# An attention and experts kernel on one core: rank products for two tiles at once, layernorms in two placed steps, a later last route, another order of the last blocks

## The chip, the cores and the metric

The kernel runs on one core of one Trainium2 chip, in fp32. The metric is the device time of one execution in microseconds (us), as a median over runs. One execution was also recorded by the hardware profiler; all durations of single instructions come from it.

The engines are called as in the profile: PE is TensorE (matmuls and transposes; PEld are its weight loads), DVE is VectorE, ACT is ScalarE, POOL is GpSimd, SP issues most DMAs.

## The reference

`x` holds 2048 tokens of 256 channels. The result is two residual layers one after the other (cut to what matters; `layernorm` has no weights where none are shown):

```python
x = x + layernorm(long_block(layernorm(x)))
x = x + layernorm(experts(layernorm(x)))

def long_block(x):                                  # 16 heads of 16 channels
    h  = layernorm(x) * ln1w + ln1b
    xc = silu(causal_depthwise_conv(h, conv_w, 4 taps) + conv_b)
    q, k = l2norm(h @ Wq), l2norm(h @ Wk)           # per head
    v = layernorm(h @ Wv) * vnw + vnb               # per head
    u = sigmoid(xc @ Wig + big) * k * v
    mem = scan(m = gamma * m + u), gamma = sigmoid(xc @ Wg + bg)    # over the tokens
    o = (layernorm(mem) * mnw + mnb) * q            # per head
    o = (layernorm(o) * gnw + gnb) * sigmoid(xc @ Wog + bog)
    h = x + o @ Wo
    h2 = layernorm(h) * ln2w + ln2b
    return h + (silu(h2 @ Wgate) * (h2 @ Wval)) @ Wout              # 1024 inner channels

def experts(x):                                     # 8 experts of 176 inner channels, the best 2 of each token
    shared = (silu(x @ sw_gate) * (x @ sw_up)) @ sw_down            # 704 inner channels
    top_w, top_i = top_k(softmax(x @ router_w.T), 2); top_w /= sum(top_w)
    routed = sum over j of top_w[j] * expert[top_i[j]](x)
    return routed + sigmoid(x @ shared_gate_w) * shared
```

## The kernel before

The tokens are taken in 8 blocks (`NB`) of 256, each of two tiles (`NT`) of 128 tokens. Channels are two groups (`KC`) of 128. A product in fp32 of 256 columns is two PE instructions of 0.216 us. The kernel has three stages.

**Attention and perceptron (0 to about 418 us).** The work of a block is cut into generators, each of which does one step and yields:

- `enter`: statistics of `x`, two scales from them by POOL's power (the reference's two layernorms in a row are one here), and `ln1` by ACT.
- `project`: the transposed `hT`, the convolution `xc`, then `q`, `k_`, `v`, their norms (`rsqrt` by bit tricks on DVE, lines 218 to 224), two POOL multiplies of `v` (L392, L393), `v` times `k_` (L395), and three gates on PE and ACT (L410).
- `remember`: transposes of `v`, the scan, transposes back, norm of `o`, two POOL operations (L449, L450), `o` times `q` (L451), and a second norm (to L459).
- `leave`: the product with `w_o`, the residual `h1`, its layernorm `ln2` and `h2T`.
- `perceptron`: eight steps `f`, each two products into a PSUM tile psM, `hid` by ACT's silu (L520) and DVE's multiply (L521), and the product of the `hid` of two steps before into the sum psD (L510). After them `h1` plus the sum, its layernorm, and `y += h1` on POOL (L531).
- `route`: layernorm `ln3` of the first layer's result, its transposes `yT`, the router's logits, the best two experts (`chosen`), the rank of each token within its expert by a product with the triangular matrix `earlier` and with `ones`, the `rows` from it, and four scatters to `xs` in DRAM by POOL (L617).
- `shared`: the expert that all tokens use: six steps into `shid` (ACT L651, DVE L652, the last half one L658), two products with `s_down`. In this stage for blocks 0 to 3.

What order these steps are issued in is written out by hand. `turns` gives every part an offset in blocks and a list of places, one for each step, in units of which a block has 8 (`NF`); all steps are sorted by `(b + first) * NF + place` and issued in that order. A block period is about 40 us. `enter` of the next block is not in the list: it is issued after a certain step of `project`, and held behind that step's last instruction. The framework's scheduler may still move single instructions; within an engine the final order is fixed, and the engine works through it in order.

**Routed blocks (to about 535 us).** `tables` and `fill` set up offsets, then `shared(4)`, then 39 `routed` blocks of 128 rows: load of `xb` from `xs`, transposes `xT` (DVE L736), products with the weights `m_w` of the expert that a register gives, and a scatter to `ys` by POOL (L765).

**The end.** `fetch` brings each token's two expert results `g` back (16 DMAs of 256 KB). PE computes `shared` of blocks 5, 6 and 7, ACT writes them to `f` with the gate. DVE adds the two weighted expert results (`combine`, L785), then comes a layernorm and the residual (`finish`, L800) and the output DMA, in the order of the blocks 0 to 7. `turn(b)` does the finish of block b-1 and then the sums of block b.

Lines 230, 231 are the statistics of any layernorm, 235 its `nb` (minus mean times scale, on DVE), 241 and 242 POOL's sum and power for the scale, 248 ACT's normalising, 285 transposes and 294 products.

## Time and profile before

| | |
|---|---|
| median of 3 runs | 592.75 us (592.64 to 594.23) |
| the profiled execution | 592.66 us |
| its span (first to last instruction) | 590.9 us |
| TensorE's granted clock, mean | 0.974 |
| PE busy | 534.9 us, 91% of the span |
| DVE, ACT, POOL busy | 327.3, 224.7, 196.8 us |

The page's second part cuts the span into 40 slices of 14.8 us, with the busy share of each engine in tenths. The waits list says which engine stood idle, for how long in total, how many times, and for what. In the timeline every row is one instruction or a run of equal ones: start, duration, engine, line, operation, output and inputs, and in brackets the idle time just before it with what ended that. The chain of waits follows the work that ended last back from the end; what stands in it sets the end. The windows give for each stretch its length, the busy time of PE, PEld, DVE, ACT and POOL with the number of instructions, then the granted clock, the DMA share and the GB/s.

### The profile page before, as it was taken

What the parts mean: (1) busy time and instruction counts of PE and PEld (TensorE: products, weight loads), DVE (VectorE), ACT (ScalarE), POOL (GpSimd) and SP (SyncE); (2) the same over time, 40 slices, a digit from 0 to 9 for tenths busy, and PEclk for the clock granted to TensorE, in tenths of its full rate; (3) what the DMA queues carried; (4) which work ended last, traced back from release to release, by engine and by line L of the source; (5) the groups of instructions that cost most, each with busy time, mean ns of one, the idle gap of its engine ahead of it and who ended that gap; (6) DMA issues with size and microseconds to landing.
All of it is one profiled execution on the core that took longest, in us unless ns stands there. A gap on an engine that the chain in (4) does not pass through costs nothing.

```text
span 590.9 us, 8088 instructions
## 1 busy us (share of the span) xinstructions
PE 534.9 (91%) x2564; PEld 448.3 (76%) x2564; DVE 327.3 (55%) x1069; ACT 224.7 (38%) x527; POOL 196.8 (33%) x307
## 2 busy tenths in 40 slices
PE   2895699999898998999999999996999999999991
PEld 1674578788787886888888888885877777768881
DVE  3588878577587586785753323223333333333684
ACT  2654353362553443543233222222223444432432
POOL 4224333324445254353412314114203333331111
PEclk9988889999999999999999999998999999999997
DMA  6940000000010010000100640001333333315311
GB/s 190 358 139 0 1 2 1 0 1 1 2 36 2 0 37 0 6 32 2 37 0 1 200 130 20 18 1 36 109 89 95 98 98 96 106 59 180 141 54 53
DMA packets 29822, 35.87 MB, mean 61 GB/s; under 512 B 4737, under 2 KB 24660, under 8 KB 29782
## 3 DMA queue, kind: packets, MB, share of 16 engines
q1 hardware_dynamic: 26082, 26.93, 14.7%
q0 software_dynamic: 3408, 8.43, 4.1%
q8 instruction: 21, 0.34, 0.3%
q14 instruction: 19, 0.16, 0.1%
q10 hardware_dynamic: 292, 0.01, 0.0%
HBM read 22.72 MB, written 13.55 MB: 61 GB/s over the span
## 4 chain that ended last, share of the span: by engine, by line
PE 34%; DVE 26%; POOL 16%; issue 11%; DMA 5%; ACT 5%; SPq 1%; POOLq 1%; ACTq 0%; DVEq 0%
PE psM L294 12%; PE psA L294 8%; PE psD L510 6%; POOL ys L765 4%; PE psS L294 4%; DVE ln_st L230 3%; DVE f L785 2%; POOL ln_rs L242 2%; DMA ys<-yb,pair 2%; POOL v L392 2%; DVE xc L359 2%; POOL v L393 2%; DVE ss L278 1%; DVE rw L222 1%; DVE rw L223 1%
## 5 line engine op out<-in xcount | busy, mean ns | idle before, releaser
L510 PE MATMUL psD<-w_out,hid 128*128 128x256 f32 x256 | 66.4, 391 | 7.7 <-DVE hid L521 7.5
L294 PE MATMUL psM<-h2T,w_gate 128*128 128x256 f32 x256 | 67.2, 385 | 0.4 <-DVE lg L570 0.4
L294 PE MATMUL psM<-h2T,w_val 128*128 128x256 f32 x256 | 65.7, 379 | 0.0
L510 PEld LDWEIGHTS psD<-w_out,hid 128*128 128x128 f32 x256 | 49.0, 194 | 18.0 <-DVE hid L521 11.5
L765 POOL DMA_INDIRECT ys<-yb,pair x39 | 38.4, 984 | 72.8 <-ACT yb L764 48.2
L294 PE MATMUL psM<-m_w,xT 128*128 x156 | 52.9, 462 | 2.4 <-DVE xT L736 2.4
L294 PEld LDWEIGHTS psM<-h2T,w_val 128*128 128x128 f32 x256 | 48.7, 190 | 7.9 <-issue 1.4
L294 PEld LDWEIGHTS psM<-h2T,w_gate 128*128 128x128 f32 x256 | 47.5, 192 | 7.1 <-DVE lg L570 1.4
L521 DVE TENSOR_TENSOR hid<-hid,psM 128x256 f32<-128x256 f32 x64 | 26.0, 413 | 37.1 <-ACT hid L520 37.1
L520 ACT ACTIVATE hid<-psM 128x256 f32<-128x256 f32 x64 | 23.8, 382 | 58.4 <-PE psM L294 58.3
L294 PE MATMUL psD<-m_w,hT 128*128 x156 | 40.2, 380 | 0.0
L617 POOL DMA_INDIRECT xs<-ln,rows x32 | 32.2, 1005 | 23.9 <-DVE rows L613 10.0
L738 DVE TENSOR_SCALAR pair<-xb,of 128x1 int32<-128x1 f32 x39 | 10.6, 272 | 48.3 <-DMA ys<-yb,pair 43.8
L294 PE MATMUL psA<-yT,s_gu 128*128 128x256 f32 x144 | 36.5, 394 | 0.0
L241 POOL TENSOR_SCALAR ln_rs<-ln_mv 128x2 f32<-128x2 f32 x24 | 6.6, 274 | 87.4 <-DVE ln_mv L231 87.3
L294 PEld LDWEIGHTS psM<-m_w,xT 128*128 128x128 f32 x156 | 26.7, 190 | 11.2 <-issue 1.5
L294 PE MATMUL psA<-xc,w_io 128*128 128x256 f32 x104 | 26.6, 401 | 5.3 <-ACT xc L363 5.1
L294 PEld LDWEIGHTS psA<-yT,s_gu 128*128 128x128 f32 x144 | 27.4, 198 | 3.3
L294 PEld LDWEIGHTS psD<-m_w,hT 128*128 128x128 f32 x156 | 26.7, 190 | 2.3 <-ACT yb L764 0.3
L749 ACT ACTIVATE padded<-psM 128x176 f32<-128x176 f32 x39 | 12.4, 317 | 41.1 <-PE psM L294 39.1
L294 PEld LDWEIGHTS psA<-xc,w_io 128*128 128x128 f32 x104 | 20.7, 201 | 8.9 <-ACT xc L363 5.9
L277 ACT ACTIVATE sq<-o 128x512 f32<-128x512 f32 x16 | 10.1, 630 | 41.5 <-DVE o L271 41.5
(233 smaller groups left out, 1128.8 us busy)
## 6 DMA issues: line engine op xcount, KB each, us to landing
xb<-xs SPq DMA_DIRECT2D x39, 129.0 KB, 2.1
g<-ys SPq DMA_DIRECT2D x16, 256.0 KB, 5.2
xs<-zeros SPq DMA_DIRECT2D x16, 129.0 KB, 5.1
x<-in_L_attn_x_dram SPq DMA_DIRECT2D x8, 256.0 KB, 3.5
out_dram<-f SPq DMA_DIRECT2D x8, 256.0 KB, 2.1
m_w<-in_L_ffn_w_gate_dram SPq DMA_DIRECT2D x2, 704.0 KB, 7.6
m_w<-in_L_ffn_w_up_dram SPq DMA_DIRECT2D x2, 704.0 KB
w_gate<-in_L_attn_Wgate_dram SPq DMA_DIRECT2D x1, 1024.0 KB, 8.1
```

The lines of the kernel that those rows point to most:

```text
L230: nc.vector.bn_stats(st[:, n, :], src[:, n, :])
L242: nc.gpsimd.tensor_tensor(rs, rs, neg_half, ALU.pow)
L294: nc.tensor.matmul(po, lhs[i], rhs[i], start=(i == 0), stop=(i == len(lhs) - 1))
L359: made = nc.vector.scalar_tensor_tensor(xc[:, k, :], hT[:, k, j : j + TB], conv_w[:, k, j : j + 1], xc[:, k, :], ALU.mult, ALU.add,)
L392: nc.gpsimd.tensor_tensor(heads(v), heads(v), over_heads(head_rows["vnw"]), ALU.mult)
L393: nc.gpsimd.tensor_tensor(heads(v), heads(v), over_heads(head_rows["vnb"]), ALU.add)
L510: nc.tensor.matmul(total[:, n * C : (n + 1) * C], hids[f][:, tok(n)], w_out[:, f, :], start=False, stop=(f == NF - 1 and n == NT - 1),)
L520: nc.scalar.activation(hid, po[:, 0:TB], AF.Silu)
L521: nc.vector.tensor_tensor(hid, hid, po[:, TB:], ALU.mult)
L617: inst = nc.gpsimd.indirect_dma_start(out=xs, out_offset=bass.IndirectOffsetOnAxis(ap=rows[:, c : c + 1], axis=0), in_=ln[:, n, :], in_off ...
L749: nc.scalar.activation(h[:, 0:I], po[:, 0:I], AF.Silu)
L765: inst = nc.gpsimd.indirect_dma_start(out=ys, out_offset=bass.IndirectOffsetOnAxis(ap=pair, axis=0), in_=yb, in_offset=None, bounds_check= ...
```

## The change

Five things are changed.

1. In `route` the rank product takes `chosen` and `seen` of both tiles at once, 16 columns in place of twice 8.
2. A layernorm is two functions: `scale_of` has the statistics and POOL's scale, `normalize` has `nb` on DVE and ACT's normalising. In `leave`, `perceptron` and `route` there is a yield between, so that each half has a place of its own. `enter` has such a yield too and becomes a part of `turns`. `v` times `k_` becomes a step of its own; `o` times `q` moves into the step after. A table `early` gives other places to a few steps of the first blocks.
3. The last block's `route` has places later by more than a unit for the transposes and what follows.
4. Three steps of `shared(5)` are issued before the routed blocks (`AHEAD`).
5. In the end phase the blocks are summed in the order 5, 0, 1, 6, 2, 3, 7, 4. For blocks 5 to 7 the experts' parts come first (the first by ACT into `f`, the second by DVE), and the shared part is added by DVE from PSUM. `finish` has two steps. The last block is finished in halves of 128 tokens, with two DVE operations in place of `nb`, ACT and an addition, and an output DMA for each half.

The core of the diff:

```diff
+    def behind(engine):
+
+        traced = nc.cur_bb.bb.instructions
+        return tc.issue_after(next(i for i in reversed(traced) if i.engine == engine))
+
+    def scale_of(part, src):
+
+        mv = stats(part, src)
+        nt = src.shape[1]
+        rs = small.tile([P, nt], F32, tag=f"rs{part}", name="ln_rs")
         nc.gpsimd.tensor_scalar(rs, mv[:, :, 1], EPS, None, ALU.add)
-        nc.gpsimd.tensor_tensor(rs, rs, neg_half, ALU.pow)
-        offset(nb, mv, rs)
-        return rs, nb
-
-    def normalize(dst, src, rs, nb):
-        for n in range(NT):
+        nc.gpsimd.tensor_tensor(rs, rs, neg_half[:, 0:nt], ALU.pow)
+        return mv, rs
+
+    def normalize(part, dst, src, mv, rs):
+
+        nt = src.shape[1]
+        nb = small.tile([P, nt], F32, tag=f"nb{part}", name="ln_nb")
+        nc.vector.scalar_tensor_tensor(nb, mv[:, :, 0], -1.0, rs, ALU.mult, ALU.mult)
+        for n in range(nt):
             nc.scalar.activation(
                 dst[:, n, :], src[:, n, :], AF.Identity, bias=nb[:, n : n + 1],
                 scale=rs[:, n : n + 1],
             )
-
-    def layernorm(part, dst, src):
-
-        rs, nb = scale_of(part, stats(part, src))
-        normalize(dst, src, rs, nb)
...
-        mv = stats("L", xt)
+        with behind(DVE) if b else ExitStack():
+            mv = stats("L", xt)
...
-        made = offset(nb, mv, inner)
-        ln = att.tile([P, NT, C], F32, tag="ln1", name=f"ln1_{b}", bufs=5)
-        normalize(ln, xt, inner, nb)
 
         nc.gpsimd.tensor_scalar(sc[:, 0, :], mv[:, :, 1], EPS, None, ALU.add)
-        nc.gpsimd.tensor_tensor(sc[:, 0, :], sc[:, 0, :], neg_half[:, 0:NT], ALU.pow)
+        nc.gpsimd.tensor_tensor(sc[:, 0, :], sc[:, 0, :], neg_half, ALU.pow)
         back = small.tile([P, NT], F32, tag="back", name=f"back_{b}", bufs=5)
         nc.gpsimd.tensor_tensor(back, va, inner, ALU.mult)
         nc.gpsimd.tensor_tensor(back, back, sc[:, 0, :], ALU.mult)
+        yield
+        ln = att.tile([P, NT, C], F32, tag="ln1", name=f"ln1_{b}", bufs=5)
+        normalize("L", ln, xt, mv, inner)
         live[b].update(ln=ln, back=back)
-        yield "entered", made
...
-        made = nc.vector.tensor_tensor(v, v, k_, ALU.mult)
-        yield "norms", made
+        yield
+        nc.vector.tensor_tensor(v, v, k_, ALU.mult)
+        yield
...
+        yield
         nc.vector.tensor_tensor(o, o, t["q"], ALU.mult)
-        yield
...
-        layernorm("B", ln, h1)
+        mv, rs = scale_of("B", h1)
+        yield
+        normalize("B", ln, h1, mv, rs)
...
-        layernorm("M", h1, h1)
+        mv, rs = scale_of("M", h1)
+        yield
+        normalize("M", h1, h1, mv, rs)
...
+    KEEP_FROM, LATE_FROM, AHEAD = 4, 5, 3
...
-        layernorm("R", ln[:, :, 0:C], x_tiles[b])
+        mv, rs = scale_of("R", x_tiles[b])
+        yield
+        normalize("R", ln[:, :, 0:C], x_tiles[b], mv, rs)
...
-        for n in range(NT):
-            product(pr[:, n * E : (n + 1) * E], [earlier, ones], [chosen[:, n, :], seen[:, n, :]])
+        product(pr[:, 0 : NT * E], [earlier, ones], [chosen, seen])
...
+            if b < LATE_FROM:
+                nc.scalar.activation(f_[:, n, :], pn, AF.Copy, scale=gate)
+            else:
+                nc.vector.scalar_tensor_tensor(
+                    f_[:, n, :], pn, gate, f_[:, n, :], ALU.mult, ALU.add
+                )
+            yield
...
-    def combine(b, g):
-
-        wt, f_ = live[b]["wt"], part_of[b]
-        for n in range(NT):
-            for j in range(TOPK):
-                nc.vector.scalar_tensor_tensor(
-                    f_[:, n, :], g[n][:, j, :], wt[:, n, j : j + 1], f_[:, n, :],
-                    ALU.mult, ALU.add,
-                )
-        mv = stats("R", f_)
-        rs = small.tile([P, NT], F32, tag="rsR", name=f"rs_{b}")
-        nb = small.tile([P, NT], F32, tag="nbR", name=f"nb_{b}")
-        nc.gpsimd.tensor_scalar(rs, mv[:, :, 1], EPS, None, ALU.add)
-        nc.gpsimd.tensor_tensor(rs, rs, neg_half, ALU.pow)
-        offset(nb, mv, rs)
-        return rs, nb
-
-    def finish(b, rs, nb):
-        f_ = part_of[b]
-        normalize(f_, f_, rs, nb)
-        nc.vector.tensor_tensor(f_, f_, x_tiles[b], ALU.add)
-        nc.sync.dma_start(in_tokens(y_out, b), f_)
+    def combine(b, n, g):
+
+        f_ = part_of[b][:, n, :]
+        for j in range(TOPK):
+            share = live[b]["wt"][:, n, j : j + 1]
+            if b >= LATE_FROM and not j:
+                nc.scalar.activation(f_, g[n][:, j, :], AF.Copy, scale=share)
+            else:
+                nc.vector.scalar_tensor_tensor(f_, g[n][:, j, :], share, f_, ALU.mult, ALU.add)
+
+    def finish(b, halves):
+
+        scales = [(hs, *scale_of("R", part_of[b][:, hs, :])) for hs in halves]
+        yield
+        for hs, mv, rs in scales:
+            f_ = part_of[b][:, hs, :]
+            normalize("R", f_, f_, mv, rs)
+            nc.vector.tensor_tensor(f_, f_, x_tiles[b][:, hs, :], ALU.add)
+            nc.sync.dma_start(in_tokens(y_out, b)[:, hs, :], f_)
+
+    def finish_last(b, n):
+
+        f_ = part_of[b][:, n : n + 1, :]
+        mv, rs = scale_of("R", f_)
+        nc.vector.tensor_scalar(f_[:, 0, :], f_[:, 0, :], mv[:, 0, 0:1], None, ALU.subtract)
+        nc.vector.scalar_tensor_tensor(
+            f_[:, 0, :], f_[:, 0, :], rs[:, 0:1], x_tiles[b][:, n, :], ALU.mult, ALU.add
+        )
+        nc.sync.dma_start(in_tokens(y_out, b)[:, n : n + 1, :], f_)
...
-        (route, 4, (0, 3.7, 4.8, 4.9, 9.2, 10.2, 10.3)),
-        (leave, 2, (0.6, 2.6, 2.8, 5.2)),
-        (remember, 1, (0.5, 2.1, 3.1, 4.1)),
-        (project, 0, (0.2, 0.3, 1.2, 1.4, 2.2, 3.1, 3.3, 3.5, 4.5, 5.5, 5.5)),
-        (perceptron, 3, (*range(NF), 7.8, 7.9)),
+        (route, 4, (1.4, 2.0, 4.2, 5.2, 5.3, 9.2, 10.2, 10.3)),
+        (leave, 2, (0.6, 2.6, 2.8, 3.6, 5.2)),
+        (remember, 1, (0.5, 2.1, 3.1, 4.3)),
+        (project, 0, (0.2, 0.3, 1.2, 1.4, 2.2, 3.1, 3.3, 4.3, 3.5, 4.5, 5.5, 5.5)),
+        (enter, -1, (3.6, 4.6)),
+        (perceptron, 3, (*range(NF), 7.8, 7.9, 8.6)),
         (shared, NB, evenly(NS + 4)),
     )
+
+    early = {(enter, 1): (0.25, 0.35), (enter, 2): (0.4, 1.3), (remember, 1): (2.5, 4.1, 5.1, 6.1)}
+    early[route, NB - 1] = (1.4, 2.0, 5.6, 6.6, 6.7, 7.9, 7.9, 7.9)
...
-        what, made = next(run, None) or (None, None)
-
-        if what == ("first", "conv", "norms")[min(b, 2)] and b + 1 < NB:
-            with tc.issue_after(made.ins):
-                next(enter(b + 1))
+        next(run, None)
...
+    late = {b: shared(b, all_banks) for b in range(LATE_FROM, NB)}
+    for _ in range(AHEAD):
+        next(late[LATE_FROM])
...
-    fetched = [fetch(b) for b in range(NB)]
-    scales = []
-
-    def turn(b):
-        if b:
-            finish(b - 1, *scales[b - 1])
-        if b < NB:
-            scales.append(combine(b, fetched[b]))
-
-    done = 0
+
+    order = (5, 0, 1, 6, 2, 3, 7, 4)
     for b in range(LATE_FROM, NB):
-        for step, (_, made) in enumerate(shared(b, all_banks)):
-            while done < b and 3 * done + 4 <= (NS + 3) * (b - LATE_FROM) + step:
-                with ExitStack() as held:
-                    for m in made:
-                        held.enter_context(tc.issue_after(m.ins))
-                    turn(done)
-                done += 1
-    for b in range(done, NB + 1):
-        turn(b)
+        new_part(b)
+    fetched = {b: fetch(b) for b in order}
+    jobs = []
+    ends = []
+    for b in order:
+        for n in range(NT):
+            jobs.append(lambda b=b, n=n: combine(b, n, fetched[b]))
+            if ends:
+                jobs.append(ends.pop(0))
+        if b < LATE_FROM:
+            run = finish(b, [slice(0, NT)])
+            ends += [lambda run=run: next(run, None)] * 2
+    jobs = iter(jobs + ends)
+
+    def work():
+        next(jobs, lambda: None)()
+
+    ends = []
+    for b in range(LATE_FROM, NB):
+        for step, _ in enumerate(late[b]):
+            for run in ends:
+                next(run, None)
+            work()
+            if step % 4 == 3:
+                work()
+            if b == NB - 1 and step > NS:
+                finish_last(b, step - NS - 1)
+        ends.append(finish(b, [slice(0, NT)]))
```

## The prediction

> **What bounds the kernel now.** I read the page's slices first, then the PE's waits, then the timeline and the chain of waits around each large gap. The profiled execution took 592.66 us (span 590.9 and 1.76 around it), the median of the three runs is 592.75: the same within 0.3% (1.8 us), which is about what a measurement of this kernel can tell from no change. So the sums are made against 592.66.
>
> ```profile
> PE 534.9 (91%) x2564; PEld 448.3 (76%) x2564; DVE 327.3 (55%) x1069; ACT 224.7 (38%) x527; POOL 196.8 (33%) x307
> PE   2895699999898998999999999996999999999991
> PEclk9988889999999999999999999998999999999997
> ```
>
> TensorE is the bound, and nothing else is near it on average. From 275 to 400 us it has no gap. So there are three sources of gain: PE work removed, PE gaps (start, 43-78, one at each block's end to 234, 406, the end), and slices at a lower clock. The PE's waits say who ends the gaps:
>
> ```profile
> PE psS L285 <- DVE v L395: 8.1, 3, 3.3
> PE psD L510 <- DVE hid L521: 7.5, 7, 1.9
> PE psA L294 <- ACT xc L363: 5.1, 1, 5.1
> PE psM L285 <- ACT ln L248: 4.6, 1, 4.6
> PE psM L294 <- DVE xT L736: 2.4, 2, 1.3
> ```
>
> The second row is the gap that recurs at a block's end. The timeline at block 2's end shows its cause:
>
> ```profile
> 185.54 0.69 DVE L395 TENSOR_TENSOR v<-v,k 128x512 f32<-128x512 f32 x1 [1.59 <-POOL v L393]
> 188.42 0.16 DVE L235 SCALAR_TENSOR_TENSOR nb<-ln_mv,sc 128x2 f32<-128x2 f32 x1 [1.02 <-POOL sc L314]
> 190.65 0.41 DVE L521 TENSOR_TENSOR hid<-hid,psM 128x256 f32<-128x256 f32 x1
> 191.12 2.33 PE L510 MATMUL psD<-w_out,hid 128*128 128x256 f32 x5 [1.87 <-DVE hid L521]
> ```
>
> DVE works in order. It waits for POOL twice (1.59 for `v`, 1.02 for the power in `enter`) with the perceptron's `hid` behind both, and PE, which has no other work issued ahead, waits for `hid`. The same picture stands at 110-113, 151 and 233 us.
>
> **Rank products (less PE work).** Eight instructions each of these rows become four with 16 columns:
>
> ```profile
> L294 PE MATMUL psM<-chosen,earlier x4: 172/256/257, 417.2 to 417.7; 128*128 128x8 f32 x4
> L294 PE MATMUL psM<-seen,ones x4: 256/256/256, 417.3 to 417.9; 128*128 128x8 f32 x4
> ```
>
> They took 0.81 us at 395.58 and 0.90 at 280.28, some 0.1 us per instruction, which is the pace of weight loads and not of columns. Half as many with doubled columns: 0.40. Gain 8 x 0.45 = **3.5 us**, all on the bound (2.0, where a gap follows the product anyway, to 3.6).
>
> **Start and first blocks.** Before, block 1's statistics stood on DVE and POOL between block 0's statistics and its `nb`: the power L314 ran at 9.95 behind block 1's `va` (8.89). With `enter` a turn of its own the power comes about 0.7 earlier, DVE's other setup ending at 10.09 allows no more: **0.7**. In 43-58 us the multiplies of `v` come ahead of `o` on POOL: `v` times `k` at about 47.5 instead of 51.19, but `o` times `q` at 51 instead of 49.6, and the silu of `xc` that ends the 5.31 us gap at 57.7 some 0.8 earlier: **0.8** (0 to 4 for both).
>
> **Block ends.** The layernorm's first half (statistics, `rs`) and second half (`nb`, ACT) become separate places, so that `nb` is issued when POOL is done; `v` times `k` is a later step, as is `o` times `q`. Moved with `enter` are per block two statistics pairs on DVE, six POOL instructions, `nb` and two ACT normalises; no DMA. Retiming block 2 by the durations of its rows: `v` times `k` at 184.85 (still waiting for POOL L393, whose place hardly moves), no wait for `nb`, the hids of f 5, 6, 7 at 187.3, 190.75 and 191.1. `hid` 6 is then late because ACT has `th` and two gates ahead of it: that is the next stall. PE ends block 2's psD at 192.9, 3.85 after f 7's products (189.08) instead of 5.24. **1.2 in each of four blocks, 4.8** (0 if ACT is fully the next wait, 9 if all gaps close).
>
> Here the Trainium skill speaks against the change. The row first: POOL's multiply of `o` and DVE's two-input operation beside it.
>
> ```profile
> 176.50 1.30 POOL L449 TENSOR_TENSOR o<-o,mnw 128x512 f32<-128x512 f32 x1 [0.94 <-DVE ss L385]
> 176.71 1.18 DVE L222 TENSOR_TENSOR rw<-rkv 128x64 f32<-128x64 f32 x1
> 179.53 0.23 DVE L222 TENSOR_TENSOR rw<-rkv 128x64 f32<-128x64 f32 x1
> ```
>
> The same DVE operation takes 1.18 beside POOL and 0.23 alone. "SBUF — State Buffer", section "Who interferes with whom", says that a DVE instruction with two SBUF inputs and a GpSimd instruction that reads SBUF shut each other out for the whole instruction. By the rule, moving DVE work ahead under POOL's two multiplies of `v` (1.28 each) blocks one such operation a block by about 1.0 and leaves 0.2 of the 1.2: the sum would be 4.0 smaller. By the row, DVE stands idle for that `v` anyway (1.59) and `hid` has only one SBUF input: I take 4.8.
>
> **The clock.** TensorE's granted clock was half from 191.3 to 194.7, and twelve psD instructions took 4.54 there instead of 2.6. "TensorE: Matmul & The Clock Gate", Part 1, "What's actually happening", gives an idle window of some 3.4 us as what halves the clock, free-running. The gap here was only 1.87 long, and gaps as long at 151 and 233 were followed by the full clock. By the rule shortening a 1.9 gap gains nothing more; by the row it gains up to 1.9. I take **1.0**.
>
> **The last route.** The chain of waits at 400-407:
>
> ```profile
> 403.45 0.96 POOL xs L617
> 404.43 0.26 POOL ln_rs L241
> 404.77 0.73 POOL ln_rs L242
> 405.72 0.61 ACT ln L248
> 406.37 0.48 PE psM L285
> ```
>
> POOL issues three scatters before block 7's `ln_rs`, and PE stands from 401.65 to 406.37 (4.72). POOL's order stays, and so does this date; but the step with ln3's transposes now comes after all six of `shared(3)`'s remaining products, about 2.5 us of PE work moved into the gap: **2.5**, with some of the half clock that follows (406.4-409.8): **0.8** (0 to 1.7). Scatters and fill behind the route start when `chosen` is there, neither earlier nor later.
>
> **Routed blocks.** Three chunks of `shared(5)` (12 products, 24 instructions of 0.216: 5.18 us) go ahead of the first expert block. Their cover is the 1.44 gap at 434.85, where PE waits for DVE's `xT`: **0.9**; the rest is only moved from the end. If the cover is gone it costs nothing, as the work is due anyhow; from 0 to 1.3, and below nothing by 0.3 if one of the three `shid` multiplies that come along (0.30 each on DVE) stands just ahead of `xT`.
>
> **The end.** Windows by stage:
>
> ```profile
> 540.00:579.00 39.00, 37.76 (x174) 32.25 (x172) 27.03 (x84) 14.44 (x33) 6.76 (x14) 1.00 0.37 133
> 579.00:591.00 12.00, 0.00 (x0) 0.00 (x0) 4.67 (x12) 2.32 (x5) 0.92 (x2) 0.70 0.19 66
> ```
>
> PE ends at 578.83, and 12.1 us follow in which two blocks' sums, a layernorm in six waits and the output DMA (4.7 after DVE's end) stand in a row. After: the last expert block ends at T (534.62 before); the first `g` lands at T+7.9, as before. PE has 87 products of 0.432 left, 37.6 us. DVE has from the first `g` 26 weighted sums x 0.40 (10.4), six from PSUM (2.6, ACT's before), statistics 7.9, `nb` 0.9, residual adds 4.5, `shid` 4.7, the last halves 1.4: 32.4 us, against 29.7 that PE has left then. So DVE is nearly the bound, and `shid`, in order behind sums, holds up `s_down` of block 6 by about 3.3 (1.23 before). PE ends at T+40.9, then the last half's sum 0.45, statistics 0.65, the two POOL operations with their hand-overs 1.25, one multiply-add 0.45, with 1.0 of other DVE work, and the DMA 4.7: T+49.4, where it was T+56.3. That is 6.9, of which 5.18 was only moved ahead: **1.7**; I take 1.2, as the sixteen `g` now land in another order. Cost at nothing: six first sums that move to ACT against six evictions that leave it (14.44 busy of 39), and a ninth output DMA on SP, hidden behind the first half's. From -1.5 (DVE fully the bound) to +5 (no stall).
>
> Sum: 3.5 + 1.5 + 4.8 + 1.0 + 3.3 + 0.9 + 1.2 = 16.2, and 592.66 - 16.2 = **576.5 us**.
>
> **Rivals.**
> *Gains in part*: DVE bounds the end (-1.5) and ACT's `th` and gates take the place of the `nb` wait (0 instead of 4.8, no clock gain). 16.2 - 2.7 - 4.8 - 1.0 = 7.7: 585.0. For: ACT has `hid` 6 behind four others. Against: one of POOL's two waits does go.
> *All gaps close*: block ends 9, first blocks 4, clock 1.9 and 1.7, no stall at the end: about 568. Against: `v` times `k` waits for POOL still.
> *Slower*: `enter`'s six POOL instructions (187.23-189.50, 2.27 us) now stand ahead of `v`'s two multiplies. They wait for DVE's statistics; my retiming leaves 1.3 us to spare. If the statistics come late, `v` times `k` and all hids behind it come later in each of six blocks. The 11.4 us that the other parts gain are used up from 1.9 us a block. At 2.6 it gives 592.66 - 11.4 + 15.6 = 597. Against: the statistics are tied to a DVE instruction well before.
> *No change*: gaps that go come back before the next product, and the end is bounded by DVE: 592 to 593.
>
> **How the numbers follow.** Forecast 0.62 (own range 572 to 581), gains in part 0.2, all gaps 0.08, slower 0.06, no change 0.04. Faster by over 0.3%: the first three less a little, 0.88; same 0.05; slower 0.07. The range, 568 to 587, leaves out the two last and the edges.
>
> **What would show it.** Right: rank rows x16 columns with half the count; no DVE wait for `nb` at the block ends and psD gaps near 0.8; a full clock at 191; some 2 us before block 7's ln3 transposes; under 0.6 before the first `m_w`; PE waiting for `shid` of block 6; a tail of about 8.5 us. Wrong: DVE `v` waiting longer for POOL behind `va` and `sc`; a gap at 275-400 where there was none; a lower clock in 50-100 than 0.86; the last DVE work over 5 us behind PE's end.

## The result, and the profile after

The changed kernel takes 589.60 us (median of 6 runs, 586.67 to 590.57) against 593.98 for the kernel before (6 runs): a ratio of 0.9922, interval 0.9895 to 0.9950. It is faster by 0.8%, where 2.7% were forecast and 568 to 587 us was the range. The profiled execution took 589.68 us, span 587.8.

The page and the PE's longest waits of the changed kernel, some rows left out. (Its lines are numbered somewhat higher; L297 is the product, L288 the transpose, L254 a layernorm's `nb`, L526 `hid`, L398 `v` times `k`, L413 the gates.)

```profile
PE 535.8 (91%) x2532; PEld 448.7 (76%) x2532; DVE 334.5 (57%) x1071; ACT 223.5 (38%) x525; POOL 202.7 (34%) x309
PE   3894789999999998997999999998999999999992
PEclk9988879999998999998999999999999999999997
```

```profile
PE psA L297 <- ACT xc L365: 7.5, 1, 7.5
PE psS L288 <- DVE v L398: 6.3, 2, 3.3
PE psM L297 <- DVE hid L526: 4.7, 3, 3.3
PE psA L297 <- ACT gate L413: 3.2, 3, 1.2
PE psM L288 <- ACT ln L256: 2.7, 2, 2.5
PE psM L297 <- DVE xT L751: 1.1, 2, 0.8
```

The wait of psD for `hid`, 7.5 us before, is gone but for 0.4. In its place stand two that were not there: psM for `hid` (4.7) and psA for a gate (3.2), 7.9 us in sum. In the first blocks the wait for `xc` is longer, 7.5 against 5.1, and that for `v` shorter, 6.3 against 8.1; that for ln3 is shorter, 2.7 against 4.6. The clock is no better: after the first 82 us, half-clock windows lie at 183.9, 269.3 and 409.2 in this execution, and at 191.3 and 406.4 in that of the kernel before.

Milestones of the two profiled executions, times in us from the span's start, show where the forecast and the result part. (An end is the start of the last product plus 0.216. These are single executions: one half-clock window of 3.41 us more or less is worth up to half of its length, 1.7 us.)

| | before | after | difference |
|---|---|---|---|
| first transposes | 11.55 | 10.17 | -1.38 |
| end of perceptron, block 0 | 114.03 | 114.29 | +0.26 |
| block 1 | 153.99 | 153.23 | -0.76 |
| block 2 | 195.50 | 193.45 | -2.04 |
| block 3 | 235.81 | 233.42 | -2.39 |
| block 4 | 274.03 | 275.54 | +1.51 |
| block 7 | 393.85 | 395.05 | +1.20 |
| last rank product | 417.18 | 416.73 | -0.46 |
| last expert product | 534.45 | 537.34 | +2.88 |
| last PE product | 578.66 | 577.22 | -1.45 |
| end | 590.87 | 587.80 | -3.07 |

From the last rank product to the end 2.6 us are gained, as forecast (0.9, 1.2, and 0.45 of that product). From 10 us to block 4's end 2.9 are lost, where 6.6 (0.8, 4.8 and 1.0) and three rank products were to be gained. In block 2 of the kernel before, two rows of the layernorm `ln2` and of the gates read:

```profile
175.59 0.16 DVE L235 SCALAR_TENSOR_TENSOR ln_nb<-ln_mv,ln_rs 128x2 f32<-128x2 f32 x1 [0.85 <-POOL ln_rs L242]
176.79 0.81 ACT L410 ACTIVATE gate<-psA,cols 128x256 f32<-128x256 f32 x2
```

The timeline of the changed kernel in the same block:

```profile
175.66 1.26 POOL L452 TENSOR_TENSOR o<-o,mnw 128x512 f32<-128x512 f32 x1
175.71 1.23 DVE L254 SCALAR_TENSOR_TENSOR ln_nb<-ln_mv,ln_rs 128x2 f32<-128x2 f32 x1 [0.53 <-POOL ln_rs L247]
176.98 1.09 ACT L256 ACTIVATE ln<-h,ln_nb,ln_rs 128x256 f32<-128x256 f32 x2 [5.46 <-DVE ln_nb L254]
182.16 0.82 ACT L413 ACTIVATE gate<-psA,cols 128x256 f32<-128x256 f32 x2
183.03 2.92 PE L297 MATMUL psA<-xc,w_g 128*128 128x256 f32 x8 [1.24 <-ACT gate L413]
185.57 0.69 DVE L398 TENSOR_TENSOR v<-v,k 128x512 f32<-128x512 f32 x1 [1.92 <-POOL v L395]
```

Three things are to be seen. `nb` of ln2, a 128x2 operation of 0.16 us, takes 1.23 beside POOL's multiply of `o`, and ACT stands behind it. The first gate's eviction from PSUM, at 176.79 before, is at 182.16, so that both psA buffers are full and PE waits 1.24 for the third gate; the eight products after it take 2.92 us instead of 1.89, as the granted clock halves at 183.9. And `v` times `k` still waits for POOL, 1.92 us now. In block 4, where no gate held PE, the last of these came out in full (chain of waits, cut in the middle):

```profile
261.85 2.20 POOL v L394
264.05 0.07 issue
264.12 1.28 POOL v L395
265.40 0.02 issue
265.42 0.69 DVE v L398
...
268.54 0.69 DVE o L462
269.23 0.34 DVE hid L526
269.57 0.04 issue
269.62 0.80 PE psM L297
```

POOL's two operations on `v` (a multiply and an addition), then `v` times `k`, then the second norm of `o`, then `hid`, then PE: 3.3 us of waiting, and a half-clock window from 269.3 on.

### The profile page after: what moved, and what is told of

Read it like the earlier page. It is cut to its first block, busy times and chain, and to the rows that moved or that the text cites. A ratio compares the mean times of both kernels' runs of the same rounds, so it can differ in the third digit from the quotient of the medians.

```text
span 587.8 us, 8025 instructions
## 1 busy us (share of the span) xinstructions
PE 535.8 (91%) x2532; PEld 448.7 (76%) x2532; DVE 334.5 (57%) x1071; ACT 223.5 (38%) x525; POOL 202.7 (34%) x309
## 4 chain that ended last, share of the span: by engine, by line
PE 44%; DVE 24%; POOL 13%; issue 10%; ACT 4%; DMA 4%; POOLq 0%; SPq 0%; DVEq 0%
PE psM L297 17%; PE psA L297 11%; PE psD L515 6%; POOL ys L780 5%; PE psS L297 4%; POOL ln_rs L247 3%; DVE ln_st L232 3%; DVE xc L361 3%; PE psD L297 2%; PE psB L297 2%; DVE hid L526 1%; DVE mem L431 1%; DVE ln_nb L254 1%; POOL v L394 1%; DMA ys<-yb,pair 1%
## 5 line engine op out<-in xcount | busy, mean ns | idle before, releaser
L297 PE MATMUL psM<-h2T,w_gate 128*128 128x256 f32 x256 | 69.5, 394 | 4.7 <-DVE hid L526 4.7
L297 PE MATMUL psM<-h2T,w_val 128*128 128x256 f32 x256 | 66.6, 383 | 0.0
L515 PE MATMUL psD<-w_out,hid 128*128 128x256 f32 x256 | 63.7, 380 | 0.4 <-DVE hid L526 0.4
L297 PEld LDWEIGHTS psM<-h2T,w_gate 128*128 128x128 f32 x256 | 49.5, 198 | 12.4 <-DVE hid L526 5.9
L297 PEld LDWEIGHTS psM<-h2T,w_val 128*128 128x128 f32 x256 | 49.7, 194 | 8.4 <-issue 1.4
L297 PE MATMUL psM<-m_w,xT 128*128 x156 | 52.8, 461 | 1.1 <-DVE xT L751 1.1
L246 POOL TENSOR_SCALAR ln_rs<-ln_mv 128x2 f32<-128x2 f32 (+1 forms) x33 | 10.0, 304 | 119.1 <-DVE ln_mv L233 100.1
L526 DVE TENSOR_TENSOR hid<-hid,psM 128x256 f32<-128x256 f32 x64 | 26.2, 413 | 36.1 <-ACT hid L525 36.1
L297 PE MATMUL psD<-m_w,hT 128*128 x156 | 40.2, 380 | 0.0
L753 DVE TENSOR_SCALAR pair<-xb,of 128x1 int32<-128x1 f32 x39 | 10.6, 273 | 48.5 <-DMA ys<-yb,pair 44.4
L297 PE MATMUL psA<-yT,s_gu 128*128 128x256 f32 x144 | 34.7, 383 | 0.9 <-DVE shid L659 0.9
L297 PEld LDWEIGHTS psM<-m_w,xT 128*128 128x128 f32 x156 | 26.7, 190 | 9.8 <-DVE xT L751 1.0
L297 PE MATMUL psA<-xc,w_io 128*128 128x256 f32 x104 | 25.7, 400 | 7.5 <-ACT xc L365 7.5
L297 PEld LDWEIGHTS psA<-yT,s_gu 128*128 128x128 f32 x144 | 26.7, 190 | 4.3 <-DVE shid L659 1.1
L297 PEld LDWEIGHTS psA<-xc,w_io 128*128 128x128 f32 x104 | 20.4, 201 | 10.5 <-ACT xc L365 7.7
L297 PEld LDWEIGHTS psD<-m_w,hT 128*128 128x128 f32 x156 | 26.7, 190 | 2.3 <-ACT yb L779 0.3
L247 POOL TENSOR_TENSOR ln_rs<-ln_rs,neg_half 128x2 f32<-128x2 f32 (+1 forms) x33 | 25.6, 774 | 2.7
```

The source lines that it names most:

```text
L246: nc.gpsimd.tensor_scalar(rs, mv[:, :, 1], EPS, None, ALU.add)
L247: nc.gpsimd.tensor_tensor(rs, rs, neg_half[:, 0:nt], ALU.pow)
L297: nc.tensor.matmul(po, lhs[i], rhs[i], start=(i == 0), stop=(i == len(lhs) - 1))
L515: nc.tensor.matmul(total[:, n * C : (n + 1) * C], hids[f][:, tok(n)], w_out[:, f, :], start=False, stop=(f == NF - 1 and n == NT - 1),)
L526: nc.vector.tensor_tensor(hid, hid, po[:, TB:], ALU.mult)
L753: nc.vector.tensor_scalar(pair, xb[:, C + 1 : C + 2], of[:, i : i + 1], xb[:, C : C + 1], ALU.not_equal, ALU.add)
```

## The experiments

Each was run in several rounds beside the kernel before, on the same chip, but not all on one chip: runs are compared by their ratios, and differences in us below are worked out from these (x 594). The clock is the mean over a kernel's runs of the granted clock.

| run | median us | ratio to before | clock |
|---|---|---|---|
| before | 593.3 to 595.1 | 1 | 0.971 to 0.973 |
| changed kernel | 589.60 | 0.9922 (0.9895 to 0.9950) | 0.966 |
| rank_only | 592.77 | 0.9980 (0.9965 to 0.9995) | 0.971 |
| end_only | 591.33 | 0.9959 (0.9942 to 0.9977) | 0.973 |
| old_pipe | 589.13 | 0.9909 (0.9886 to 0.9932) | 0.974 |
| gate0_back | 589.34 | 0.9900 (0.9869 to 0.9931) | 0.968 |
| vk_mid | 589.40 | 0.9910 (0.9884 to 0.9935) | 0.965 |
| nb_yt | 599.83 | 1.0097 (1.0069 to 1.0126) | 0.959 |
| hid5_first | 587.51 | 0.9906 (0.9874 to 0.9939) | 0.974 |
| before_fill | 593.26 | 0.9983 (0.9970 to 0.9997) | 0.972 |
| gate0_fill | 584.98 | 0.9845 (0.9809 to 0.9880) | 0.976 |
| after_fill | 583.45 | 0.9833 (0.9809 to 0.9856) | 0.977 |
| fill_start | 587.62 | 0.9897 (0.9880 to 0.9915) | 0.974 |
| before_vdve | 587.55 | 0.9896 (0.9872 to 0.9920) | 0.974 |
| after_vdve | 576.93 | 0.9720 (0.9682 to 0.9759) | 0.977 |
| v_dve | 577.36 | 0.9736 (0.9718 to 0.9755) | 0.978 |
| vdve_last | 576.20 | 0.9707 (0.9682 to 0.9732) | 0.981 |
| vo_dve | 573.03 | 0.9657 (0.9630 to 0.9683) | 0.982 |
| after_vo | 569.06 | 0.9564 (0.9538 to 0.9590) | 0.981 |
| vo_one_out | 568.70 | 0.9570 (0.9552 to 0.9588) | 0.981 |

**The parts alone.** The rank product in the kernel before (`rank_only`):

```diff
-        for n in range(NT):
-            product(pr[:, n * E : (n + 1) * E], [earlier, ones], [chosen[:, n, :], seen[:, n, :]])
+        product(pr[:, 0 : NT * E], [earlier, ones], [chosen, seen])
```

> The kernel before with nothing changed but the rank product (both tiles in one). A: PE work comes off the bound, 8 x 0.45 = 3.6 us, and all of it is seen: ratio 0.994. B: in blocks 0 to 3 the PE gap at the block's end is set by the chain DVE, POOL, DVE and not by PE, so the products of blocks 0 to 2 (which are issued in those blocks) give nothing, 5 x 0.45 = 2.2 us: ratio 0.9962.

B was nearer, and still too high: it expected 0.9962. The rows show the saving in PE's work itself: four instructions in 0.36 us instead of eight in 0.81, at each of the eight places (tile list of the changed kernel):

```profile
L297 PE MATMUL psM<-chosen,earlier x2: 179/220/262, 416.7 to 416.8; 128*128 128x16 f32 x2
L297 PE MATMUL psM<-seen,ones x2: 262/262/263, 416.9 to 417.0; 128*128 128x16 f32 x2
```

But the kernel gains 1.2 us (0.2%), not 3.6. In the profiled executions the stretch from block 3's end to block 7's is what got shorter, from 158.05 to 156.87 us, with no wait of PE over 0.7 us in it. The products of blocks 0 and 1 are followed by a wait for `hid` (at 191 and 234), that of block 6 by the wait for ln3, whose date POOL sets.

The end alone (`end_only`: three `shared(5)` steps ahead, the last blocks' new order) and everything but the first stage's order (`old_pipe`: `enter` to `perceptron` as before, and the places):

```diff
-        (enter, -1, (3.6, 4.6)),
...
+        (route, 4, (0, 0, 3.7, 4.8, 4.9, 9.2, 10.2, 10.3)),
+        (leave, 2, (0.6, 2.6, 2.8, 5.2)),
+        (remember, 1, (0.5, 2.1, 3.1, 4.1)),
+        (project, 0, (0.2, 0.3, 1.2, 1.4, 2.2, 3.1, 3.3, 3.5, 4.5, 5.5, 5.5)),
...
+    early = {(route, NB - 1): (1.4, 2.0, 5.6, 6.6, 6.7, 7.9, 7.9, 7.9)}
```

> The kernel before with only the new end: three steps of the shared expert ahead of the routed blocks and the last blocks' new order. A: as forecast and as the milestones of the two traces say (from the last rank product to the end 2.6 us less, 0.45 of it the rank product): 2.1 us less, ratio 0.9965, tail after PE's last product about 10.5 us. B: the gain at the end comes from work that the earlier gaps had moved: nothing, ratio 1.000.

> The changed kernel with the order of the first stage as before (layernorms in one step, enter behind project's steps, old places), but with the rank products for two tiles, block 7's route later, three steps ahead of the routed blocks and the new end. A: the new order of the first stage costs more than it brings (milestones: 1.5 us later at block 4's end though three rank products were saved), so this is faster than the changed kernel by about 3 us: ratio 0.987. B: the order is worth what was forecast for it (7.3 us): this is slower than the changed kernel, ratio about 1.00. C: the order makes no difference, ratio 0.992.

The end is worth 2.4 us (0.0041 x 594), A. `old_pipe` is as fast as the whole change, C by time: 5.4 us (0.0091) below the kernel before, so that 1.8 are left for block 7's later route, if the parts add up; no run has that part alone. But `old_pipe` has clock 0.974 where the change has 0.966. Time multiplied by mean clock, as a rough measure of the time at full clock, is 573.8 for `old_pipe`, 569.2 for the change and 577.7 for the kernel before: by this measure the new order saves some 4.6 us, and the clock takes as much.

**Places of the first stage.** `gate0_back` corrects one number. The list of places is sorted, but a generator does its steps in order; so `v` times `k`, listed at 4.3, was issued at 3.5, and the first gate, listed at 3.5, at 4.3.

```diff
-        (project, 0, (0.2, 0.3, 1.2, 1.4, 2.2, 3.1, 3.3, 4.3, 3.5, 4.5, 5.5, 5.5)),
+        (project, 0, (0.2, 0.3, 1.2, 1.4, 2.2, 3.1, 3.3, 3.5, 3.5, 4.5, 5.5, 5.5)),
```

> The changed kernel with the first gate's product back at place 3.5 (it had 4.3, because a part's steps run in their order while its places are sorted, so that v times k took 3.5 and the gate 4.3). A: ACT's eviction of that gate comes before the squares of o again, both psA buffers are not full together, and PE's waits for the gate (0.83, 1.41, 1.41 at 143, 183 and 223 us) go, with the half clock at 183: some 4 to 5 us below the changed kernel, ratio to before about 0.985. B: PE only reaches the wait for hid earlier, which DVE's chain from v to o sets: the gaps move to psD or psM and the time is that of the changed kernel within 1 us, ratio 0.992.

The waits for the gate went, and a new one came before the router's logits, of 1.2 to 2.0 us in each of four blocks (its waits and timeline):

```profile
PE psM L297 <- ACT yT L570: 6.8, 4, 2.0
```

```profile
179.01 0.63 ACT L280 ACTIVATE sq<-o 128x512 f32<-128x512 f32 x1 [2.08 <-DVE o L274]
179.55 0.57 ACT L570 COPY yT<-psM 128x512 f32<-128x512 f32 x1
180.17 1.01 PE L297 MATMUL psM<-w_r,yT 128*128 128x9 f32 x6 [1.83 <-ACT yT L570]
```

ACT waits for DVE's `o` with `yT` behind it. The time is unchanged: B in effect, with the gap before psM as it said, though PE waits there for `yT` and not for `hid`. `vk_mid` issues `v` times `k` after the first gate:

```diff
-        nc.vector.tensor_tensor(v, v, k_, ALU.mult)
-        yield
...
             gates.append(t)
             yield
+            if j == 0:
+                nc.vector.tensor_tensor(v, v, k_, ALU.mult)
+                yield
...
```

> The changed kernel with v times k issued after the first gate (gate at 3.5, v times k at 4.3: the places as they stand in the list, one for each step). It differs from the run with the gate back only in that v times k is later in DVE's order. A: as with the gate back, and DVE has the second norm of o ahead of v times k while POOL multiplies v, so that hid of step 5 comes up to 1 us earlier: ratio 0.982. B: hid of step 5 is still behind both, nothing more is gained than with the gate back. C: v is late for the next block's transposes: slower by 1 us than with the gate back.

The same time again, B. `nb_yt` moves two places more, and `hid5_first` on top of that `remember`'s last step and `v` times `k`:

```diff
-        (route, 4, (1.4, 2.0, 4.2, 5.2, 5.3, 9.2, 10.2, 10.3)),
-        (leave, 2, (0.6, 2.6, 2.8, 3.6, 5.2)),
+        (route, 4, (1.4, 2.0, 3.4, 5.2, 5.3, 9.2, 10.2, 10.3)),
+        (leave, 2, (0.6, 2.6, 2.8, 3.0, 5.2)),
```

```diff
-        (remember, 1, (0.5, 2.1, 3.1, 4.3)),
+        (remember, 1, (0.5, 2.1, 3.1, 5.2)),
...
+            if j == 1:
+                with behind(DVE):
+                    nc.vector.tensor_tensor(v, v, k_, ALU.mult)
+                yield
```

> The run with the gate back, with two places moved: ln2's second half at 3.0 (ahead of o times its scale, and so of POOL's two multiplies of o) and the transposes to yT at 3.4, so that ACT copies yT before it waits for the squares of o. A: the port is what delays nb (1.23 instead of 0.16 us beside POOL's multiply of o) and with it ACT's queue; nb takes 0.16 again, PE's waits for yT (1.4, 2.0, 2.0, 2.1) go, and with them two or three half-clock windows of 1.7 us: 584 us, ratio 0.983. B: the gap moves on to the wait for hid behind v times k, as in the kernel before (2.0 a block): 589, ratio 0.991.

> As the run before, and on DVE the multiply for hid of step 5 ahead of v times k and of the second norm of o (v times k is issued after the second gate and held behind DVE's last instruction, the fourth step of remember is placed at 5.2). A: the waits of DVE for POOL with hid behind them are the one cause of the gaps at the block ends; PE has no gap over 0.6 us from block 1 to 4: 2 us a block less than before in four blocks, the clock stays full: 580 to 582 us, ratio 0.978. B: another in-order queue (ACT: gates and h2T ahead of silu) takes the place: 587, ratio 0.988.

`nb_yt` is slower than the kernel before by 1%, which neither theory said. Its timeline in block 2:

```profile
180.82 1.18 DVE L223 TENSOR_TENSOR rw<-rkv 128x64 f32<-128x64 f32 x1
189.65 0.69 DVE L398 TENSOR_TENSOR v<-v,k 128x512 f32<-128x512 f32 x1 [1.59 <-POOL v L395]
192.53 0.16 DVE L254 SCALAR_TENSOR_TENSOR ln_nb<-ln_mv,sc 128x2 f32<-128x2 f32 x1 [0.93 <-POOL sc L318]
194.34 0.41 DVE L526 TENSOR_TENSOR hid<-hid,psM 128x256 f32<-128x256 f32 x1
194.81 0.79 PE L297 MATMUL psM<-h2T,w_gate 128*128 128x256 f32 x1 [4.36 <-DVE hid L526]
```

With ln2's `nb` early, POOL's operations on `o` fall on the `rsqrt` of `k` and `v` instead (1.18), `enter`'s statistics slip behind `v` times `k`, and both old waits for POOL stand in one row ahead of `hid`. In `hid5_first` `hid` is ahead of `v` times `k`, and PE still waits 1.5 to 2.0 us a block, now for `hid` behind `enter`'s `nb`: B's time, with POOL in front and not ACT. None of these reorderings removed the wait: each put another of the POOL operations in front.

**The clock.** Seven products of zeros into the running sum fill PE's waits and add nothing (`gate0_fill` on `gate0_back`, `after_fill` on the changed kernel; `before_fill` has them ahead of `down(5)` in blocks 1 to 3):

```diff
+            if f == 5 and 1 <= b <= 4:
+                for _ in range(7):
+                    nc.tensor.matmul(total, nothing[:, 0:P], nothing, start=False, stop=False)
```

> The run with the gate back, with seven products of zeros into the running sum (7 x 0.216 = 1.5 us of PE work that adds nothing) ahead of the router's logits in blocks 1 to 4, where PE otherwise stands idle for 1.4 to 2.1 us. A: the clock gate looks at PE's activity, so idle stretches well under 3.4 us can cost a half-clock window, and filling them saves it: mean clock from 0.967 to about 0.975, time 3 to 5 us below the run with the gate back, ratio 0.984. B: what halves the clock has nothing to do with these gaps: same clock, and the same time or up to 1 us more.

> The changed kernel with seven products of zeros into the running sum (1.5 us of PE work that adds nothing) ahead of the router's logits in blocks 1 to 4, and nothing else changed: they lie some 1.7 us ahead of PE's wait for the third gate (0.8 to 1.4 us in blocks 1 to 3). A: what took back the new order's gain is the clock: the half-clock windows near 184 and 270 us go, mean clock from 0.966 to 0.972 or more, time 3 us below the changed kernel: ratio 0.987. B: the clock falls because of what the gaps' place is and not their length: clock and time as of the changed kernel, ratio 0.992, or up to 2 us more where the products do not fit into a wait.

> The kernel before with seven products of zeros ahead of the last steps' sums in blocks 1 to 3, where PE waits 2.0 us for hid. A: the one window in three that those waits cost goes: clock from 0.9725 to 0.975, 1.5 us less, ratio 0.9975. B: nothing.

In the first two A holds, and `after_fill` gives more than was expected of it: PE does 1.5 us more in each of four blocks, and the changed kernel becomes 0.9% faster. So the gaps cost it more than their own length: the clock goes from 0.966 to 0.977. The stage's windows without them (`gate0_back`) and with them (`gate0_fill`):

```profile
175.00:200.00 25.00, 23.17 (x114) 20.17 (x113) 20.50 (x61) 12.17 (x29) 10.39 (x18) 0.93 0.00 1
```

```profile
175.00:200.00 25.00, 24.33 (x125) 20.00 (x124) 21.18 (x62) 12.10 (x29) 11.07 (x19) 1.00 0.00 1
```

The third number from the end is the clock. In the kernel before (`before_fill`) the gain is 1 us, at the limit of what can be told. `fill_start` put such products into the first 80 us as well and ahead of ln3 of block 7:

```diff
+    fl0 = psum("D")
+    for _ in range(14):
+        warmed = nc.tensor.matmul(fl0, zeros_b[:, 0:P], zeros_b, start=True, stop=True).ins
...
+        for n in (6, 16, 7):
+            with behind(PE):
+                for _ in range(n):
+                    nc.tensor.matmul(fl, zeros_b[:, 0:P], zeros_b, start=True, stop=True)
+            yield
...
```

> The run with the gate back and the products of zeros in blocks 1 to 4, with more of them: 14 from the first microseconds until the weights for the first transposes are there, 6, 16 and 7 in the waits of the first blocks (3.1, 7.9 and 3.5 us near 30, 57 and 71 us) and 8 ahead of block 7's ln3 transposes (2.7 us near 404). A: the full clock comes near 10 us instead of 17 to 20, and the half-clock windows at 30, 51-62, 72-79 and 404 us (some 24 us) go: mean clock about 0.995, and as PE in the first 80 us often waits for others, 5 us less than that run: ratio 0.976. B: the ramp is bound by DVE, ACT and POOL alone: no gain but the 1.7 at 404, ratio 0.982.

Neither holds: it is slower than `gate0_fill` by 3 us. The window at 404 went, but the products at the start moved the order of the setup on DVE and PE, which then waited 4.0 us for `cols`, and block 0 ended 2.3 us later; so it says nothing of what a full clock is worth in the ramp.

**The path through POOL.** The two operations on `v` by DVE, in the changed kernel (`after_vdve`) and before (`before_vdve`); with `o`'s two as well (L452 and L453, in the same way), `after_vo`:

```diff
-        nc.gpsimd.tensor_tensor(heads(v), heads(v), over_heads(head_rows["vnw"]), ALU.mult)
-        nc.gpsimd.tensor_tensor(heads(v), heads(v), over_heads(head_rows["vnb"]), ALU.add)
+        nc.vector.tensor_tensor(heads(v), heads(v), over_heads(head_rows["vnw"]), ALU.mult)
+        nc.vector.tensor_tensor(heads(v), heads(v), over_heads(head_rows["vnb"]), ALU.add)
```

> The changed kernel with the two operations on v by DVE in place of POOL, nothing else. A: the path DVE, POOL, DVE to v times k kept the forecast gain away: the gaps at 143 to 288 us and in the first blocks shrink by 1.5 us each and most half-clock windows go: 578 to 580 us, ratio 0.975. B: the clock was the larger part, and without the products of zeros the windows stay: 585, ratio 0.986.

> The kernel before with the two operations on v by DVE. A: one of its two waits for POOL at each block's end goes (1.6 us) and the first blocks' gaps shrink: 4 x 1.3 and 4 to 5 us in the first blocks, 584, ratio 0.983; the wait for enter's power stays, so that the new places are worth some 4 us more than before on top of it. B: the wait for enter's power takes all of it, as the statistics come earlier but the power follows them: 590, ratio 0.993.

> The changed kernel with the two operations on v and the two on o by DVE in place of POOL, nothing else (no products of zeros, the first gate where the change put it). A: with nb of ln2 at 0.16 us again ACT reaches the gates 1 us earlier and PE's waits for the third gate (0.8 to 1.4) shrink below 0.5; no half-clock window between 80 and 390 us: 573 to 574 us, ratio 0.966. B: the first gate's late place keeps those waits: 575 to 577 us, ratio 0.970.

`after_vdve` gains 12 us on the changed kernel (0.0202), and reaches 576.9: A. About half of it, by time multiplied by clock (569.2 to 563.5), is there at full clock; the rest came with the clock, 0.977 instead of 0.966. `before_vdve` gains 6, between its A and B: what is left there is the other wait, for `enter`'s power, with a PE gap of 1.2 to 2.1 us a block:

```profile
186.78 0.16 DVE L235 SCALAR_TENSOR_TENSOR nb<-ln_mv,sc 128x2 f32<-128x2 f32 x1 [0.81 <-POOL sc L314]
190.57 1.78 PE L510 MATMUL psD<-w_out,hid 128*128 128x256 f32 x7 [1.77 <-DVE hid L521]
```

So the change is worth 4.6 us with `v` on POOL (0.0078) and 10.5 without (0.0176). Some 5.4 of either belong to the parts that `old_pipe` has too, if these count the same in both. What the new order of the first stage brings is thus nothing while `v` is on POOL and some 5 us once it is on DVE: the one wait hides what the removal of the other is worth. `after_vo` is faster than A said, 4.4% below the kernel before. In its profile `nb` is short again, `o` takes 0.69 on DVE, and block 2 has neither a gap nor a low clock:

```profile
167.19 0.16 DVE L254 SCALAR_TENSOR_TENSOR ln_nb<-ln_mv,ln_rs 128x2 f32<-128x2 f32 x1 [0.53 <-POOL ln_rs L247]
167.26 0.69 DVE L452 TENSOR_TENSOR o<-o,mnw 128x512 f32<-128x512 f32 x1
175.86 0.68 DVE L398 TENSOR_TENSOR v<-v,k 128x512 f32<-128x512 f32 x1
```

```profile
175.00:200.00 25.00, 25.00 (x127) 22.00 (x126) 19.19 (x67) 13.13 (x29) 9.56 (x16) 1.00 0.05 17
```

The step from `after_vdve` to `after_vo` gives DVE two operations a block more, 11 us over the kernel, and DVE's busy time falls from 340.6 to 336.7 us: by these figures some 15 us (an estimate) had gone into operations that took longer beside POOL's work on `o`. `v_dve`, `vdve_last` and `vo_dve` are the same steps on `gate0_fill`:

> The run with the gate back and the products of zeros, with the multiply and the addition on v by DVE (0.69 each) in place of POOL (1.59 and 1.27). A: the path from DVE to POOL and back to v times k is what holds hid of step 5; it is 1.5 us shorter, and no port is shared there: any wait for hid in blocks 1 to 4 goes, 1 to 2 us below the run it starts from, ratio 0.982. B: those waits are hidden once the products of zeros are there, and DVE (18 to 21 of 25 us busy in these blocks) has 1.4 us a block more in its queue, which delays xc, hid or the statistics: 2 to 6 us slower than that run, ratio 0.990 to 0.995.

> The run with v on DVE and the products of zeros in blocks 1 to 4 (ratio 0.9736), and eight such products ahead of block 7's ln3 transposes, in the gap of 2.7 us. A: the half-clock window that followed this gap in most runs goes: 1.0 to 1.7 us less, ratio 0.9715. B: that run's profile had no window there anyway, so no change: 0.9736.

> As the run before, with the two operations on o by DVE as well (1.4 us of DVE instead of 2.6 on POOL, beside which DVE's two-input operations take 1.1 to 1.3 us instead of 0.2). A: the shared port costs DVE about as much as doing the work itself, so DVE's queue gets no longer and ln2's nb comes 1 us earlier: 1 us less, ratio 0.970. B: DVE is now full in blocks 1 to 4 and hid waits: 2 to 5 us more, ratio 0.976 to 0.98.

A's direction in `v_dve` and `vo_dve`, with more than A said: 6.5 us where 1 to 2 were expected, and 3.0 where it was 1. `vdve_last` shows no difference that its interval can tell. With the path gone the products of zeros and the gate's place are no longer needed: `after_vo` has neither and is 5.5 us (0.0093) faster than `vo_dve`.

**The last DMA.** `vo_one_out` is `after_vo` with the last block's output written at once:

```diff
-        nc.sync.dma_start(in_tokens(y_out, b)[:, n : n + 1, :], f_)
+        if n == NT - 1:
+            nc.sync.dma_start(in_tokens(y_out, b), part_of[b])
```

> The changed kernel with v and o on DVE (ratio 0.9564), and the last block's output in one DMA of 256 KB after both halves in place of two of 128 KB. A: the ninth output DMA costs 1.5 us at the program's end: 4.67 us from DVE's last operation to the end, 1.5 us less: ratio 0.954. B: the 6.19 us do not depend on it: the same or 0.3 us more for the larger last transfer, ratio 0.9565.

B: nothing changes. What sets the end is told below.

## Why the prediction was wrong, point by point

Of the 16.2 us forecast, 4.6 came. If the parts add up, the rank products brought 1.2 (forecast 3.5), the routed blocks and the end 2.4 (2.1), block 7's later route 1.8 (3.3), and the new order of the first stage, with its clock, nothing that can be told (0.8 lost), where 7.3 (1.5, 4.8 and 1.0) were to be gained.

*Block ends (4.8 forecast).* This is the step that failed. It retimed DVE with `v` times `k` "still waiting for POOL L393, whose place hardly moves", took one of two waits away, and gave PE 1.2 us a block for it. PE's wait did not shrink: 7.5 us for `hid` before, 4.7 for `hid` and 3.2 for a gate after, as the other wait, and ACT's queue, filled the room. One sign that it named for being wrong came: `v` waits longer for POOL, 1.92 us in block 2 instead of 1.59, though not behind `va` and `sc`. `after_vdve` shows the price of the path through POOL that was left: 12 us over all blocks and the ramp, its clock included.

*The rule on the shared port.* The working set the rule beside the row and took the row's side, because DVE was idle for `v` and `hid` has one SBUF input. By the rule it would have said 580.5, nearer, though not near enough. The operation that met POOL was another, `nb` of ln2 beside the multiply of `o`: 1.23 instead of 0.16 us, with ACT and the gates behind it. So an operation a block was blocked by about 1 us, as the rule has it, and its place was looked for at `v` alone. `after_vo` against `after_vdve` puts some 9 us on `o` (0.0156 of the time). That move ends the meeting at the port and the way to POOL and back at once; no run parts the two.

*The gate's place.* Not seen: the sorted places exchange `v` times `k` and the first gate. Putting it back alone was worth nothing measurable (`gate0_back`).

*The clock (1.0).* It was counted as a gain, and by the rule it cites as nothing; it was a loss. Windows went from one in the blocks to two, and the mean clock from 0.972 to 0.966. By milestones, block 4's 3.9 us loss is a 3.3 gap and the window at its end.

*Rank products (3.5).* The size was right, 0.45 each; "all on the bound" was wrong: 1.2 alone. The working named the case ("where a gap follows the product anyway") and put what is left then at 2.0.

*Start and first blocks (1.5).* The first transposes came 1.4 us earlier; by 30 us that was gone, as the full clock was granted at 20.1 us instead of 17.2 in these two executions. The silu of `xc` came 0.6 later instead of 0.8 earlier: `v` times `k`, at 48.1 nearly as worked out, took 1.75 us beside POOL's multiply of `o`, and then `o`, `hn_sum` and `xc` take turns on DVE behind POOL's `o`.

*The last route (3.3).* The gap shrank from 4.6 to 2.5 us by the waits, nearly as worked out, but the half-clock window stayed. Between the end of block 7 and the last rank product 1.7 us were gained, 0.45 of it by block 6's rank product.

*Routed blocks and the end (0.9 and 1.2).* Right in sum: 2.6 between the milestones, 0.45 of it a rank product, and 2.4 in `end_only`. But the tail is 10.6 us and not 8.5, while PE's own wait there was 1.3 and not 3.3: two misses of 2 us that cancel, which is luck.

*Rivals.* "Gains in part" gave the place rightly (the wait for POOL, then ACT), with 585.0; its size was short by the clock, the first blocks and the ranks. The sum of "All gaps close" is off: its own terms give 564, as an end without a stall was put in at 1.2 instead of 5.

## What to carry to other kernels

Where an in-order queue meets two waits for another engine, price the removal of both, and try first to do the waited-for work on the engine that waits: two operations of 0.7 us a block more on DVE made the kernel before 6 us faster and the changed one 12. A product that costs less PE time gains only where PE isn't about to wait. And once gaps are about 2 us long, look at the granted clock of every stage before comparing orders: an order that is better by some 4.6 us at full clock, by a rough measure, measured the same.

## What the runs showed of the hardware

*The clock halves after short gaps.* PE's idle stretches of 1.8 to 2.2 us in blocks 1 to 4 were followed by a half-clock window, mostly of 3.41 us, in 13 of 24 cases over eight profiles, one of 1.24 us (at 183 in the changed kernel) as well; none of under 1 us was. Which of the 24 it hits, no run shows. The Trainium skill, "TensorE: Matmul & The Clock Gate", Part 1, "What's actually happening", names an idle window of about 3.4 us: here less was enough, and the measurement decides. Products of zeros count as activity: with them the windows of `gate0_back` at 181, 222 and 263 us were gone. The full clock was first granted between 16.8 and 20.1 us, save where products of zeros ran from 1.9 us on: 6.8 there, and lost again at 10.2, where PE waited.

*The port.* A DVE operation of 0.16 or 0.23 us took 1.1 to 1.3 beside POOL's 512-element multiply, and POOL's own took 1.6 or 2.2 instead of 1.27 beside one or two of DVE's. The Trainium skill, "SBUF — State Buffer", "Who interferes with whom", has a DVE instruction with two SBUF inputs and a GpSimd instruction that reads SBUF contend in this way, and agrees.

*The program's end.* The last rows of POOL, before and after:

```profile
583.45 0.71 POOL L793 TENSOR_TENSOR rs<-rs,neg_half 128x2 f32<-128x2 f32 x1
```

```profile
580.52 0.57 POOL L247 TENSOR_TENSOR ln_rs<-ln_rs,neg_half 128x1 f32<-128x1 f32 x1
```

Each program ends 6.71 us after this row (584.16 to 590.87, 581.09 to 587.80), and so do the other eighteen profiled runs, while the time from DVE's last operation to the end is 4.67 in some and 6.19 in others. POOL's closing drain, which begins beside that row, took 6.65 and 6.51 us. So the tail goes by POOL's last operation, and the forecast's "DMA 4.7" after DVE's end became 6.19. That the drain is the cause is not shown: putting the last power on another engine wasn't tried.
